# VectorE's SBUF passes ahead of its PSUM passes, GpSimd's pieces beside the latter, in a basic block's convolutions

## The chip, the core and the metric

The kernel runs on one core of a Trainium2 chip. The metric is the device time of one execution in microseconds. TensorE (PE) multiplies matrices into PSUM; PEld is its loading of weights. VectorE (DVE), ScalarE (ACT) and GpSimd (POOL) work element by element; SyncE (SP) issues most of the transfers. Each engine goes through its own list of instructions in order, and instructions on different engines wait for each other by semaphores.

## The reference

An input x of 2 images, 128 channels, 128 x 128 pixels, float32, goes through four layers: a 3x3 convolution followed by a small Mamba scan over channel groups, group norm and a residual (layer 0); a density gate (layer 1); layer 0's form again with other weights (layer 2); and a basic block with signs of weights (layer 3). Only the last is touched by the change:

```python
w1b = w1 + lax.stop_gradient(jnp.sign(w1) - w1)
w2b = w2 + lax.stop_gradient(jnp.sign(w2) - w2)
out = jax.nn.relu(_batchnorm(_conv3x3(x, w1b), gamma1, beta1))
out = _batchnorm(_conv3x3(out, w2b), gamma2, beta2)
out = out + x
return jax.nn.relu(out)
```

Batch norm takes mean and variance over both images and all pixels, so the second convolution can't begin before the first is complete.

## The kernel before, in words

Channels lie on the 128 partitions. The first 6900 us or so are layers 0 to 2. Then comes the basic block, the function `_basic_block`. It keeps the whole result of a convolution, Y, in SBUF (2 x 128 x 128 floats per partition), and runs over 32 bands of 8 rows (16 per image).

A band is convolved by Winograd's method along the rows: four output rows come from six input rows, so six transformed inputs, each convolved along the width with three taps, give four outputs. Four parts of the code do this for a band k:

- `edges(k)`: from the ten rows of the band (tile `band`, in one of three fixed buffers, `room`), VectorE makes four combinations (L889, each "-4 times one row set plus another", both inputs in SBUF) into slots 0, 3, 2 and 5 of a new tile `comb` (three buffers). GpSimd makes the differences: L890 into slots 1 and 4 out of the band, L891 into slots 0 and 5 out of the four combinations, L892 into slot 3.
- `rest_of(v)`: VectorE finishes `comb` in place with L897 (slot 4 from 1 and 4), L898 (slot 1, reading what L897 wrote) and L899 (slot 2, reading slot 3 of L892), all inputs in SBUF.
- `products(v)`: TensorE multiplies the six slots by the transformed weights u, 18 matmuls in the program (36 in the trace, L906), into a PSUM tile m of three banks (two buffers).
- `conv(m, ...)`: ScalarE copies a third of m to SBUF (c, L917). VectorE forms sums and differences of m and c (two L921, two L922, one pair into an SBUF tile and one pair into a PSUM tile, both named sd), and then the output rows in Y: L926 from m and the SBUF pair, and L927 to L930, each with the PSUM pair as one operand and an SBUF tile as the other. Two bn_stats passes over Y (L932) end it.

In L897 to L899 and L889 both inputs lie in SBUF; in L921 to L930 one lies in SBUF and the other in PSUM; L932 has a single input in SBUF.

`convolve(load, make, n)` runs this for one convolution, as a pipeline over steps k with the order of every engine written out by hand (a block of `tc.manual_schedule`). Step k holds, before the change: the rest of band k+1 (`rest_of`), the products of band k, the conv of band k-1, the load of band k+4, the making of band k+3, and the edges of band k+2 with their differences. The arguments load and make differ by convolution:

- In the first, `load` sets a border row to zero by a GpSimd memset where the image ends (L879, L881), and SyncE issues two transfers, the scan's output y into `band` (L974) and the layer's input into `xs` (L976, two buffers). `residual` makes the band: Silu with the group norm's scale and bias on ScalarE (L982), the residual's addition on GpSimd (L983, two SBUF inputs), and a transfer of the sum to `x3` in DRAM by SyncE (L984).
- In the second there is nothing to load. `normalised` sets the border, lets GpSimd copy two rows from the band before (L995), and ScalarE applies batch norm's scale and bias with a Relu to rows of Y (L997).

A third loop after both, the output pass, loads x3, adds the second convolution's result (L1010), applies Relu (L1011) and stores. It isn't touched.

Of the kernel before, what the change touches and what calls it, by code (L numbers as in the profile page):

```python
# [27 lines left out]
ALU = mybir.AluOpType  # L28
# [14 lines left out]
BAND = 8  # L43
# [776 lines left out]
def _basic_block(tc, src, y, norm, x3, scratch, w1, w2, bn, out, B, H):  # L820
# [7 lines left out]
    nc = tc.nc  # L828
    fours = BAND // 4
    with tc.tile_pool(name="bb", bufs=1) as cp, tc.tile_pool(name="bband", bufs=2) as bp, tc.tile_pool(  # L830
# [3 lines left out]
        def combined():  # L834
            return bp.tile([P, 6, fours, P + 2], F32, tag="comb", name="comb", bufs=3)
# [33 lines left out]
        bands = [(b, r0) for b in range(B) for r0 in range(0, H, BAND)]  # L869

        def span(k):

            r0 = bands[k][1]
            return room[k % 3], 1 if r0 == 0 else 0, BAND + 1 if r0 + BAND == H else BAND + 2
# [8 lines left out]
        def edges(k):  # L883

            xb = span(k)[0]
            v = combined()
            low, high = [xb[:, n : n + BAND, :].rearrange("p (i n) w -> p n i w", n=4) for n in (0, 2)]
            for n, at in enumerate((0, 3, 2, 5)):
                nc.vector.scalar_tensor_tensor(v[:, at], low[:, n], -4.0, high[:, n], ALU.mult, ALU.add)  # L889
            nc.gpsimd.tensor_tensor(v[:, 1:5:3], high[:, 1:3], low[:, 1:3], ALU.subtract)  # L890
            nc.gpsimd.tensor_tensor(v[:, 0:6:5], v[:, 2:6:3], v[:, 0:4:3], ALU.subtract)  # L891
            nc.gpsimd.tensor_tensor(v[:, 3], v[:, 2], v[:, 3], ALU.add)  # L892
            return v

        def rest_of(v):
            x = [v[:, n].rearrange("p i w -> p (i w)") for n in range(6)]
            nc.vector.scalar_tensor_tensor(x[4], x[1], -2.0, x[4], ALU.mult, ALU.add)  # L897
            nc.vector.scalar_tensor_tensor(x[1], x[1], 4.0, x[4], ALU.mult, ALU.add)  # L898
            nc.vector.scalar_tensor_tensor(x[2], x[2], 2.0, x[3], ALU.mult, ALU.subtract)  # L899

        def products(v):

            m = pp.tile([P, 3, 2, fours, P], F32, tag="m", name="m")
            for n, i in enumerate((2, 4, 3, 1, 0, 5)):
                for kw in range(3):
                    nc.tensor.matmul(  # L906
                        m[:, n // 2, n % 2],
                        lhsT=u[:, i, kw, :],
                        rhs=v[:, i, :, kw : kw + P],
                        start=(kw == 0),  # L910
                        stop=(kw == 2),
                    )
            return m

        def conv(m, b, r0, stats):
            c = bp.tile([P, 2, fours, P], F32, tag="c", name="c")
            nc.scalar.copy(c, m[:, 0])  # L917
            sd1 = bp.tile([P, 2, fours, P], F32, tag="sd", name="sd", bufs=1)
            sd2 = pp.tile([P, 2, fours, P], F32, tag="sd", name="sd")
            for n, sd in enumerate((sd1, sd2)):  # L920
                nc.vector.tensor_tensor(sd[:, 0], m[:, 1, n], c[:, n], ALU.add)  # L921
                nc.vector.tensor_tensor(sd[:, 1], m[:, 1, n], c[:, n], ALU.subtract)  # L922
            rows = Y[:, b, r0 : r0 + BAND, :]
            y = rows.rearrange("p (i n) w -> p n i w", n=4)
            (s1, d1), (s2, d2) = [(sd[:, 0], sd[:, 1]) for sd in (sd1, sd2)]
            nc.vector.tensor_tensor(y[:, 0:4:3], m[:, 2], sd1, ALU.add)  # L926
            nc.vector.scalar_tensor_tensor(y[:, 1], d2, 2.0, d1, ALU.mult, ALU.add)  # L927
            nc.vector.scalar_tensor_tensor(y[:, 2], s2, 4.0, s1, ALU.mult, ALU.add)
            nc.vector.tensor_tensor(y[:, 0], s2, y[:, 0], ALU.add)
            nc.vector.scalar_tensor_tensor(y[:, 3], d2, 8.0, y[:, 3], ALU.mult, ALU.add)  # L930
            for n in range(BAND // ROWS):
                nc.vector.bn_stats(  # L932
                    stats[:, (b * H + r0) // ROWS + n, :],
                    rows[:, n * ROWS : (n + 1) * ROWS, :].rearrange("p r w -> p (r w)"),
                )

        def affine(stats, n):
            mv = cp.tile([P, 2], F32, tag=f"mv{n}", name="mv")
            nc.vector.bn_aggr(mv, stats.rearrange("p a b -> p (a b)"))
            rstd = _rstd(nc, cp, mv[:, 1:2], BN_EPS, f"bn{n}")  # L940
            return _affine(nc, cp, mv[:, 0:1], rstd, bnc[:, 2 * n : 2 * n + 1], bnc[:, 2 * n + 1 : 2 * n + 2], f"bn{n}")
# [4 lines left out]
        def convolve(load, make, n):  # L946

            stats = cp.tile([P, B * H // ROWS, 6], F32, tag="st", name="st")
            v = {}
            E = mybir.EngineType  # L950
            with tc.manual_schedule(engines={E.PE, E.Activation, E.DVE, E.Pool, E.SP}):
                m = {}
                for k in range(-4, len(bands) + 1):
                    if 0 <= k + 1 < len(bands):
                        rest_of(v[k + 1])
                    if 0 <= k < len(bands):
                        m[k] = products(v.pop(k))
                    if k >= 1:
                        conv(m.pop(k - 1), *bands[k - 1], stats)
                    for ahead, f in ((4, load), (3, make)):  # L960
                        if 0 <= k + ahead < len(bands):
                            f(k + ahead)
                    if 0 <= k + 2 < len(bands):
                        v[k + 2] = edges(k + 2)
            return affine(stats, n)

        rests = {}
# [10 lines left out]
        def residual(k):  # L978
# [5 lines left out]
            nc.sync.dma_start(out=x3[b][:, r0 : r0 + BAND, :], in_=xb[:, 1 : BAND + 1, 1 : P + 1])  # L984

        s1, t1 = convolve(load, residual, 0)


# [11 lines left out]

        nc.sync.dma_start(out=u.rearrange("p a t c -> p (a t c)"), in_=later)
        s2, t2 = convolve(lambda k: None, normalised, 1)

        for k, (b, r0) in enumerate(bands):
# [90 lines left out]
```

## Time and profile before

The median of three runs is 7705.66 us (7701.60 to 7708.43). The profiled execution took 7677.97 us, and its span from the first to the last instruction is 7676.1 us, at a mean granted TensorE clock of 0.926.

| stretch of the span, us | what | PE busy | DVE busy | POOL busy | ACT busy | granted clock | GB/s |
|---|---|---|---|---|---|---|---|
| 0 to 7676.1 | all | 6354.0 | 7120.0 | 5563.7 | 4278.8 | 0.926 | 230 |
| 6900 to 7274 | first convolution | 278.5 | 343.9 | 201.5 | 65.9 | 0.90 | 165 |
| 7274 to 7575 | second convolution | 258.9 | 273.2 | 127.4 | 55.7 | 0.96 | 6 |
| 7575 to 7676 | output pass | 0 | 43.5 | 0 | 36.4 | 0.50 | 306 |

Some durations in the basic block, means from the groups by shape: L889 420 ns, L897 422, L921 413, L926 680, L932 685 on VectorE; L890 1451, L891 1406, L892 801, L983 2692 on GpSimd. The three L897 to L899 have the same shape as L889.

How to read it: busy time counts an instruction from its start to its end, also when it stands still in between, so the mean of a group against that of another of the same shape tells whether it does. In a group's row, after the shapes and the count, stand the busy time in us, the mean in ns, and after the second bar the idle time of the engine just before these instructions, with what ended it. In the timeline the columns are the start, the duration, engine, line, operation, and tiles; in brackets the engine's idle time before it and what it waited for.

### The profile page before, as it was taken

Reading aid. Unit: us, or ns where it says so; the run is one execution under the profiler, and the core shown is the slowest. Engines: PE = TensorE matmul, PEld = TensorE weight load, DVE = VectorE, ACT = ScalarE, POOL = GpSimd, SP = SyncE. Lnnn points to the kernel's source line nnn. Section 1 sums busy time; section 2 is a strip of 40 time slices with the busy share of each in tenths; the row PEclk is TensorE's granted clock in tenths of the full one; section 3 lists DMA queues with packets and bytes.
Section 4 is the critical chain, followed back from the end, with each engine's and each line's share of the span. In section 5 each row is a group of like instructions: output and inputs, shape, how many; then the busy total and the mean of one; then the engine's idle time right before and its main releaser. Section 6 shows DMA issues by size and latency. Waiting matters only on the chain.

```text
span 7676.1 us, 89472 instructions
## 1 busy us (share of the span) xinstructions
PE 6354.0 (83%) x30416; PEld 2345.8 (31%) x30416; DVE 7120.0 (93%) x7082; ACT 4278.8 (56%) x4877; POOL 5563.7 (72%) x1815
## 2 busy tenths in 40 slices
PE   7888888888888888867888888888888888877793
PEld 2222222222222222234222222222222222226673
DVE  6999999999999999966899999999999999999996
ACT  5666666666665666555566666666566666641112
POOL 5777877778777787743877777777777888765541
PEclk9999999999999999868999999999999999988897
DMA  7999999999999999944999999999999999975404
GB/s 207 252 248 249 254 251 255 245 249 250 253 247 248 252 252 254 246 180 150 245 258 246 246 251 248 254 249 248 246 252 249 248 256 255 251 201 181 129 1 170
DMA packets 573737, 1769.79 MB, mean 231 GB/s; under 512 B 85568, under 2 KB 239712, under 8 KB 458208
## 3 DMA queue, kind: packets, MB, share of 16 engines
q1 hardware_dynamic: 568672, 1747.28, 86.6%
q10 hardware_dynamic: 4608, 16.78, 0.6%
q8 instruction: 242, 3.96, 0.2%
q14 instruction: 215, 1.76, 0.1%
HBM read 1552.83 MB, written 210.89 MB: 230 GB/s over the span
## 4 chain that ended last, share of the span: by engine, by line
DVE 49%; DMA 22%; PE 12%; issue 7%; ACT 4%; POOL 4%; SPq 1%; POOLq 0%; DVEq 0%; ACTq 0%
DMA bcr<-sb 16%; DVE set L472 15%; DVE h L477 13%; DVE r L473 12%; DMA ur<-su 3%; PE set L454 2%; PE one L350 2%; POOL h L445 2%; ACT set L463 2%; PE one L400 2%; PE ys L492 1%; DVE v L505 1%; DVE comb L899 1%; PE ys L483 1%; POOL comb L891 1%
## 5 line engine op out<-in xcount | busy, mean ns | idle before, releaser
L445 POOL TENSOR_TENSOR h<-ur,bcr 128x2048 f32<-128x2048 f32 x896 | 4060.2, 4539 | 1141.8 <-DMA bcr<-sb 951.9
L472 DVE TENSOR_TENSOR set<-set,h 128x1024 f32<-128x1024 f32 x1792 | 2192.9, 1224 | 263.5 <-ACT set L463 161.8
L473 DVE TENSOR_TENSOR r<-set,bcr 128x1024 f32<-128x1024 f32 x1792 | 2194.1, 1224 | 61.4
L463 ACT ACTIVATE set<-set 128x1024 f32<-128x1024 f32 x1792 | 1746.3, 1006 | 887.1 <-PE set L454 876.1
L477 DVE TENSOR_TENSOR h<-set,h 128x1024 f32<-128x1024 f32 x1536 | 1864.0, 1214 | 24.0 <-POOL h L445 23.6
L454 PE MATMUL set<-dt,rep 32*128 32x512 f32 x7168 | 1405.3, 674 | 102.3 <-DVE h L477 96.1
L492 PE MATMUL ys<-r,ct 128*32 128x512 f32 x7168 | 1175.3, 635 | 35.6 <-DVE r L473 35.5
L323 PE MATMUL one<-band,conv 128*128 128x512 f32 x2304 | 1081.2, 605 | 22.0 <-DMA band<-in_x_dram 12.6
L454 PEld LDWEIGHTS set<-dt,rep 32*128 32x128 f32 x7168 | 404.3, 193 | 1002.7 <-issue 458.5
L400 PE MATMUL one<-xc,keep 128*64 128x512 f32 x1008 | 322.4, 723 | 457.6 <-ACT xc L357 355.8
L906 PE MATMUL m<-comb,u 128*128 128x256 f32 x2304 | 537.4, 394 | 137.3 <-DVE Y L926 90.8
L323 PEld LDWEIGHTS one<-band,conv 128*128 128x128 f32 x2304 | 406.5, 189 | 668.3 <-issue 596.7
L483 PE MATMUL ys<-t,ct 128*128 128x512 f32 x512 | 325.8, 722 | 251.9 <-DVE v L505 250.4
L906 PEld LDWEIGHTS m<-comb,u 128*128 128x128 f32 x2304 | 449.8, 197 | 224.6 <-issue 100.3
L492 PEld LDWEIGHTS ys<-r,ct 128*32 128x32 f32 x7168 | 181.7, 112 | 938.9 <-issue 767.5
L352 ACT ACTIVATE xc<-one,keep 128x512 f32<-128x512 f32 x252 | 173.4, 688 | 513.3 <-PE one L350 508.3
L374 POOL TENSOR_TENSOR u<-dt,xc 128x1024 f32<-128x1024 f32 x128 | 302.8, 2366 | 130.8 <-ACT dt L368 130.5
L420 PE MATMUL one<-prod,ct 128*128 128x512 f32 x504 | 278.1, 634 | 98.2 <-POOL prod L412 63.2
L350 PE MATMUL one<-y,w_in 128*128 128x512 f32 x504 | 343.1, 770 | 1.6 <-ACT xc L352 1.6
L463 ACT ACT_TABLE_LOAD x254 | 325.9, 1283 | 4.5
L917 ACT COPY c<-m 128x512 f32<-128x512 f32 x64 | 37.5, 586 | 517.9 <-PE m L906 292.2
L364 PE MATMUL one<-xc,w_dt 128*128 128x512 f32 x504 | 312.1, 704 | 2.7 <-ACT bc L407 2.7
(166 smaller groups left out, 6323.9 us busy)
## 6 DMA issues: line engine op xcount, KB each, us to landing
ur<-su SPq DMA_DIRECT2D x896, 896.0 KB, 11.4
bcr<-sb SPq DMA_DIRECT2D x896, 448.0 KB, 11.5
ur<-su SPq DMA_DIRECT2D x896, 128.0 KB, 11.0
su<-u SPq DMA_DIRECT2D x1024, 64.0 KB, 3.3
sb<-bc SPq DMA_DIRECT2D x256, 224.0 KB, 2.6
bcr<-sb SPq DMA_DIRECT2D x896, 64.0 KB, 10.7
y<-o SPq DMA_DIRECT2D x128, 256.0 KB, 9.1
band<-in_x_dram SPq DMA_DIRECT2D x28, 640.0 KB, 11.0
```

The source lines that it names most:

```text
L323: nc.tensor.matmul(py.rearrange("p (r w) -> p r w", r=ROWS), lhsT=w["conv"][:, tap, :], rhs=xb[:, r + kh : r + kh + ROWS, kw : kw + P], st ...
L350: nc.tensor.matmul(p, lhsT=w[("in", "z")[i]][:, g, :], rhs=s["y"], start=True, stop=True)
L400: nc.tensor.matmul(p[g * NQ * DS : (g + 1) * NQ * DS, :], lhsT=w[("xb", "xcm")[i]], rhs=s["xc"][:, g, :], start=True, stop=True,)
L445: nc.gpsimd.tensor_tensor(b, s["ur", t], s["bc", t][:, 0].unsqueeze(1).to_broadcast([P, NJ, NS]), ALU.mult)
L454: nc.tensor.matmul(a[j // 2][:, j % 2, :], lhsT=w["rep"][r, q, :], rhs=s["dt"][r, g, :], start=True, stop=True, tile_position=(r.start, 0),)
L463: nc.scalar.activation(x, x, AF.Exp)
L472: nc.vector.tensor_tensor(pt, pt, s["h", t - 1][:, js, :], ALU.mult)
L473: nc.vector.tensor_tensor(s["r", t][:, js, :], pt, s["bc", t - 1][:, 1].unsqueeze(1).to_broadcast([P, 2, NS]), ALU.mult)
L477: nc.vector.tensor_tensor(s["h", t][:, js, :], pt, s["h", t][:, js, :], ALU.add)
L483: nc.tensor.matmul(s["ys", g], lhsT=con["ident"], rhs=s["t1"][:, g, :], start=True, stop=False)
L492: nc.tensor.matmul(s["ys", g][a : a + NQ * DJ, :], lhsT=red[:, q, :], rhs=r[:, j, :], start=False, stop=(q == NQ - 1), tile_position=(0, a),)
L906: nc.tensor.matmul(m[:, n // 2, n % 2], lhsT=u[:, i, kw, :], rhs=v[:, i, :, kw : kw + P], start=(kw == 0), stop=(kw == 2),)
```

## The change

In `convolve`, the edges of band k+2 move from the end of a step to just behind the rest of band k+1, ahead of the products and the conv. GpSimd's three differences are taken out of `edges` into a function of their own, `differences`, which is called after the conv and ahead of the load and the making; inside it, the difference over the band alone (L890) comes last instead of first. So VectorE's order in a step becomes L897, L898, L899, four times L889, then L921 to L932; GpSimd's becomes L891, L892, L890, then border and L983 (or L995). Nothing is computed differently.

```diff
             for n, at in enumerate((0, 3, 2, 5)):
                 nc.vector.scalar_tensor_tensor(v[:, at], low[:, n], -4.0, high[:, n], ALU.mult, ALU.add)
-            nc.gpsimd.tensor_tensor(v[:, 1:5:3], high[:, 1:3], low[:, 1:3], ALU.subtract)
+            return v
+
+        def differences(k, v):
+            xb = span(k)[0]
+            low, high = [xb[:, n : n + BAND, :].rearrange("p (i n) w -> p n i w", n=4) for n in (0, 2)]
             nc.gpsimd.tensor_tensor(v[:, 0:6:5], v[:, 2:6:3], v[:, 0:4:3], ALU.subtract)
             nc.gpsimd.tensor_tensor(v[:, 3], v[:, 2], v[:, 3], ALU.add)
-            return v
+            nc.gpsimd.tensor_tensor(v[:, 1:5:3], high[:, 1:3], low[:, 1:3], ALU.subtract)
...
                     if 0 <= k + 1 < len(bands):
                         rest_of(v[k + 1])
+                    if 0 <= k + 2 < len(bands):
+                        v[k + 2] = edges(k + 2)
                     if 0 <= k < len(bands):
                         m[k] = products(v.pop(k))
                     if k >= 1:
                         conv(m.pop(k - 1), *bands[k - 1], stats)
+                    if 0 <= k + 2 < len(bands):
+                        differences(k + 2, v[k + 2])
                     for ahead, f in ((4, load), (3, make)):
                         if 0 <= k + ahead < len(bands):
                             f(k + ahead)
-                    if 0 <= k + 2 < len(bands):
-                        v[k + 2] = edges(k + 2)
```

## The prediction

> **What bounds the kernel now.** The page gives VectorE (DVE) 93% of the span busy, the most of all engines, and the changed functions run in its last five slices. So I cut it to these: the busy time of each engine over the first convolution, the second, and the output pass (columns: stretch, length, busy us of PE, PEld, DVE, ACT, POOL with instruction counts, granted clock, DMA share, GB/s).
>
> ```profile
> 6900.00:7274.00 374.00, 278.48 (x1152) 231.25 (x1152) 343.89 (x597) 65.89 (x67) 201.53 (x136) 0.90 0.52 165
> 7274.00:7575.00 301.00, 258.92 (x1152) 218.54 (x1152) 273.19 (x587) 55.66 (x65) 127.38 (x129) 0.96 0.02 6
> ```
>
> DVE is busy for 92% and 91% of the two convolutions. Whether it works or stands in a lock shows in the groups by shape, here from 6945 to 7255 us (count, busy us, mean ns):
>
> ```profile
> L899 DVE SCALAR_TENSOR_TENSOR comb<-comb 128x260 f32<-128x260 f32 x28 | 71.6, 2557 | 17.6 <-POOL comb L892 17.6
> L889 DVE SCALAR_TENSOR_TENSOR comb<-band 128x260 f32<-128x260 f32 x116 | 41.5, 420 | 0.0
> L898 DVE SCALAR_TENSOR_TENSOR comb<-comb 128x260 f32<-128x260 f32 x28 | 39.1, 1397 | 1.0
> L897 DVE SCALAR_TENSOR_TENSOR comb<-comb 128x260 f32<-128x260 f32 x28 | 11.8, 422 | 0.0
> ```
>
> One operation, one shape, and 420, 1397 or 2557 ns. The timeline of one step says why:
>
> ```profile
> 7026.42 1.40 POOL L891 TENSOR_TENSOR comb<-comb 128x520 f32<-128x520 f32 x1 [4.98 <-DVE comb L889]
> 7026.71 1.40 DVE L898 SCALAR_TENSOR_TENSOR comb<-comb 128x260 f32<-128x260 f32 x1
> ...
> 7027.90 0.80 POOL L892 TENSOR_TENSOR comb<-comb 128x260 f32<-128x260 f32 x1
> 7028.66 2.67 POOL L983 TENSOR_TENSOR band<-band,xs 128x1280 f32<-128x1280 f32 x1
> 7028.73 2.89 DVE L899 SCALAR_TENSOR_TENSOR comb<-comb 128x260 f32<-128x260 f32 x1 [0.63 <-POOL comb L892]
> ...
> 7031.30 1.47 POOL L890 TENSOR_TENSOR comb<-band 128x520 f32<-128x520 f32 x1
> ...
> 7031.55 0.41 DVE L921 TENSOR_TENSOR sd<-m,c 128x256 f32<-128x256 f32 x1
> ```
>
> L898 ends 0.29 us after POOL's L891, L899 0.29 us after POOL's L983: each stood still until GpSimd was done. L921, with one operand in PSUM, takes its usual 0.41 us beside L890. One step at the image border shows the other passes beside the long L983:
>
> ```profile
> 7051.49 2.90 POOL L983 TENSOR_TENSOR band<-band,xs 128x1280 f32<-128x1280 f32 x1
> ...
> 7053.22 0.68 DVE L926 TENSOR_TENSOR Y<-m,sd 128x512 f32<-128x512 f32 x1
> ```
>
> L926's mean is 680 ns, so nothing was lost; the next L890 ran over L929, L930 and L932, which took 0.41, 0.41 and 1.29 for the pair, as always. There L899 came 0.08 us ahead of L983, and that step took 8.88 us instead of 11.34. In the second convolution TensorE waits a little in each step:
>
> ```profile
> 7442.57 8.01 PE L906 MATMUL m<-comb,u 128*128 128x256 f32 x36 [1.04 <-DVE Y L926]
> 7451.61 8.01 PE L906 MATMUL m<-comb,u 128*128 128x256 f32 x36 [1.03 <-DVE Y L926]
> ```
>
> So a step is 11.34 us in the first convolution and 9.04 in the second, set by DVE with its stalls; TensorE needs 8.01.
>
> **What the Trainium skill says.** "SBUF — State Buffer", section "Who interferes with whom": a DVE instruction with two SBUF inputs contends with a GpSimd instruction that reads SBUF, and whichever issues second is blocked until the first ends; with at most one SBUF input (outside the two-port modes) it doesn't contend. The trace agrees: 2.89 us for L899 against L983's 2.67, and 0.41 for L921. "TensorE: Matmul & The Clock Gate", Part 1: idleness throttles the matrix clock. The trace agrees in kind: after idle gaps of about 3.3 us a step's 36 matmuls took up to 9.7 or 10.75 us, after gaps of 1.67 us or less always 8.01.
>
> **The change, part by part.** No instruction is added or removed; the order on DVE and POOL and the neighbours change. Start-to-start spacings on DVE, from the timeline: four L889 1.35 us, L897 to the L898 that reads it 0.46, L898 and L899 0.34 each uncontended, and a whole conv (L921 to the end of its place) 4.69. Sum 7.18. The rest of 11.34 is stall: L898 and the wait for L892 take 2.02 instead of 0.34, L899 2.82 instead of 0.34, together 4.16. In the second convolution L899 meets only the short L995, and the stalls are 1.86.
>
> *Edges ahead of conv, differences beside it.* Let E be the end of the four L889. POOL then starts L891 0.08 later (as now), L892 1.49 after that, L890 0.76 later, and after 1.45 the add L983 (2.67): it ends at E+6.45. DVE meanwhile runs conv from E-0.08 to E+4.62, all passes with at most one SBUF input, so nothing is lost by the overlap. The former stalls of L898 and the 0.63 wait for L892 are gone.
>
> *What is late next, first convolution.* The add L983 now lies behind all three differences, and DVE reaches L897 at E+4.62, while L983 holds the read port until E+6.45. So 1.83 us of stall remain. L897 ends 0.30 after L983 (as L899 does now), then 0.04, 0.34, 0.34 and 1.43 to the new E: 6.45+0.30+2.15 = 8.90 us a step. Edges must also wait for this L983 now (before, its band was finished 16 us earlier): it is the same instant, no further cost. The loop is DVE edges, POOL differences and add, DVE rest and edges.
>
> *TensorE in it.* L926 ends at E+2.06 and frees PSUM for products at E+2.2; 8.01 fits in 8.90 with 0.9 idle, short of what cools the clock. There is one new wait: edges comes ahead in the step, so its buffer (one of three) is the one that products(k-1) has yet to give back. Queued behind edges on DVE is conv, which TensorE needs two products later. In the first convolution those matmuls end some 6 us before edges; costs nothing.
>
> *The queues.* On POOL the border memsets and the add go behind the differences; three memsets of 0.20 enter the chain, and three shorter adds give 0.7 back. On SP nothing is reordered, but the store of x3 and the next two loads now go out together at L983's end: store 3.2, y 4.3 and xs 5.5 us to landing now, 1.79 MB per step, 201 GB/s at 8.90 against 165 now and up to 255 elsewhere on the page. They are needed two steps later at E+3.8, some 15 us after issue, Silu's 1.46 included for y; even the slowest seen there (8.64) fits.
>
> *First convolution, sum.* Edges(0) ends about 6916 (a weight pass, L853, no longer stands behind the second add); three rounds of 8.90 bring E of band 3 to 6942.7 (now 6947.0), 28 more bring band 31 to 7191.9 (now 7255.2). The tail is longer, since edges leads by more: products(30) runs E+2.2 to 10.2, products(31) to 18.2, then copy 0.6 and conv 4.79: 23.7 us against 18.5. The statistics end at 7215.6 instead of 7273.7: 58.1 us saved.
>
> *Second convolution.* POOL needs 0.08+1.49+0.76+1.45+0.4, DVE 7.18, TensorE 8.01: TensorE becomes the bound. With T the end of products(k-1), edges runs T+0.1 to 1.5, conv's L926 ends at T+3.6, far ahead of T+8, and rest ends at T+7.3; the new buffer wait costs DVE 0.7 us of idleness a step and TensorE nothing. Now 284.3 us pass from the first matmul (7284.91) to the last (7569.21). After: first products 10.43 (cold, as now) plus 31 x 8.01 = 258.7, so 25.6 less; the first products start 0.9 later, because all three differences stand ahead of the first rest. Saved: 24.7.
>
> The output pass and all before 6900 us stay. Sum 82.8: span 7676.1 becomes 7593.3. The profiled execution took 7678.0, the median of the runs shown is 7705.7; I take the difference off the median: **7623 us**, 1.07% faster.
>
> What the trace doesn't show is a long stretch of matmuls with no gap. Its bounds: 8.01 x 31, or a clock a little lower, as the first 10.43 over 8.01 shows it can be; 8.4 a step would cost 12 us. I take 8.01, since from 7300 to 7320 TensorE is busy all 20 us at clock 1.00.
>
> **Rivals.**
> 1. *The first convolution keeps a longer loop* (landings late through SP, or matmuls that cool down): some 9.7 to 10.5 us a step, each added 1.0 taking back 29 us. Saved 37 to 60: 7645 to 7669. For it speaks that store and loads now share the DMA queues; against it the 5 us of slack.
> 2. *The add doesn't stall DVE* as reckoned, and TensorE's 8.01 binds both: 28 x 0.89 more, 107 saved, about 7598. Against it: L899 behind L983 in nearly every step now.
> 3. *Slower: conv's passes are held while GpSimd reads*. Then POOL's 6.45 and DVE's 4.69 and 2.49 come one after another: 13.6 a step, and 4.2+4.69+2.49 = 11.4 in the second; +64 and +69, about 7839. It decides once conv is held over 2.4 us a step in the first. L921, L926, L929, L930 and L932 beside POOL at their usual times speak against it; a wait written for a whole tile, which would do the same, can't be excluded.
> 4. *The change only moves the stall*: DVE loses behind L983 what it gains on L891. This would need 4 us of stall behind L983; it has only 2.67.
>
> **How the numbers follow.** My forecast 0.70 (own range 7608 to 7640: 0.3 us a step and startup each way), rival 1 0.14, rival 2 0.07, rival 3 0.06, rival 4 0.03 (no change). Within 0.2%, about 15 us, a measurement can't tell this kernel from no change. Faster 0.91, same 0.03, slower 0.06. The range takes in the forecast and most of rivals 1 and 2: 7598 to 7654.
>
> **What would show it.** L898 and L899 at 0.42 us; L897 at up to 2.2 us in the first convolution, ending 0.3 after L983; L889 starting every 8.9 us, then every 8.0; L921 to L932 unchanged; matmuls of the second convolution without gaps, clock 1.00. I am wrong if conv's passes lengthen beside POOL, if ACT's Silu waits for landings, or if L889 waits for L906 for over a microsecond in the first convolution.

## The result, and the profile after

The changed kernel took 7594.4 us (median of four runs, 7579.2 to 7596.2), the kernel before 7707.1 in the same comparison; the ratio is 0.9849, 95% interval 0.9832 to 0.9866. Repeated on one chip (first experiment below) it was 0.9882, 0.9867 to 0.9898: 97 us. The profiled execution took 7595.0 us, with a span of 7593.2.

The lines of `after` are shifted against before: L897 to L899 (rest) are now L901 to L903; the differences L891, L892, L890 are L895, L896, L897, in that order; conv's L921, L926 and L932 are L925, L930 and L936; the matmuls L906 are L910; the addition L983 is L989.

Stretches of the changed kernel, with the columns used before (length, busy us of PE, PEld, DVE, ACT, POOL, granted clock, DMA share, GB/s): first convolution, second convolution.

```profile
6900.00:7215.00 315.00, 265.44 (x1176) 221.53 (x1173) 293.03 (x620) 70.09 (x70) 189.84 (x136) 0.93 0.64 197
7215.00:7492.00 277.00, 253.69 (x1162) 221.34 (x1160) 239.08 (x598) 57.49 (x67) 115.34 (x129) 0.96 0.03 11
```

The groups by shape in the first convolution (6950 to 7190 us): count, busy us, mean ns, idle time ahead.

```profile
L989 POOL TENSOR_TENSOR band<-band,xs 128x1280 f32<-128x1280 f32 x26 | 69.8, 2684 | 0.0
L901 DVE SCALAR_TENSOR_TENSOR comb<-comb 128x260 f32<-128x260 f32 x28 | 51.5, 1840 | 3.5 <-POOL comb L897 3.5
L889 DVE SCALAR_TENSOR_TENSOR comb<-band 128x260 f32<-128x260 f32 x112 | 40.4, 423 | 0.0
...
L897 POOL TENSOR_TENSOR comb<-band 128x520 f32<-128x520 f32 x28 | 36.3, 1296 | 0.0
L895 POOL TENSOR_TENSOR comb<-comb 128x520 f32<-128x520 f32 x28 | 36.1, 1288 | 72.5 <-DVE comb L889 72.5
...
L902 DVE SCALAR_TENSOR_TENSOR comb<-comb 128x260 f32<-128x260 f32 x28 | 12.0, 429 | 1.0
L903 DVE SCALAR_TENSOR_TENSOR comb<-comb 128x260 f32<-128x260 f32 x28 | 11.8, 422 | 0.0
...
L933 DVE TENSOR_TENSOR Y<-sd,Y 128x256 f32<-128x256 f32 x27 | 11.2, 413 | 0.0
```

Where before two passes of the rest stood still (1397 and 2557 ns), now one does, the first, at 1840; the other two take 0.42 us. GpSimd's pieces became shorter too: L895 1288 ns against 1406, L897 1296 against 1451. One step in the timeline:

```profile
7082.32 2.68 POOL L989 TENSOR_TENSOR band<-band,xs 128x1280 f32<-128x1280 f32 x1
...
7083.48 1.81 DVE L901 SCALAR_TENSOR_TENSOR comb<-comb 128x260 f32<-128x260 f32 x1
...
7086.01 1.44 DVE L889 SCALAR_TENSOR_TENSOR comb<-band 128x260 f32<-128x260 f32 x4
...
7087.60 1.29 POOL L895 TENSOR_TENSOR comb<-comb 128x520 f32<-128x520 f32 x1 [2.59 <-DVE comb L889]
...
7088.97 0.73 POOL L896 TENSOR_TENSOR comb<-comb 128x260 f32<-128x260 f32 x1
...
7089.66 1.30 POOL L897 TENSOR_TENSOR comb<-band 128x520 f32<-128x520 f32 x1
...
7090.91 2.69 POOL L989 TENSOR_TENSOR band<-band,xs 128x1280 f32<-128x1280 f32 x1
...
7092.08 1.81 DVE L901 SCALAR_TENSOR_TENSOR comb<-comb 128x260 f32<-128x260 f32 x1
```

L901 starts 1.16 us after the addition starts and ends 0.29 us after it has ended: 7083.48+1.81 against 7082.32+2.68. From one L989 to the next pass 8.59 us. Conv's passes lie beside GpSimd's pieces and keep their times (L933 413 ns; the same pass, L929, had 412 before). In the second convolution TensorE has no gaps left; the timeline of PE shows all 32 products as one row:

```profile
7234.31 251.67 PE L910 MATMUL m<-comb,u 128*128 128x256 f32 x1152 [17.30 <-DVE comb L903]
```

I split the span at the last group norm's aggregation (L604) and at the two batch norms' aggregations. The part from L604 to the end, "the block", holds all that the change touches.

| us | ahead of the block | first convolution | second | output pass | block |
|---|---|---|---|---|---|
| before | 6891.6 | 382.2 | 300.9 | 101.4 | 784.5 |
| changed | 6909.9 | 312.6 | 269.0 | 101.7 | 683.3 |

The block is 101.2 us shorter. The part ahead, where both kernels do the same, is 18.3 us longer in this profile: so the spans differ by just 82.9 us, which is by chance the sum that the prediction had.

### The profile page after: what moved, and what is told of

It is laid out like the page before. It is cut to its first block, busy times and chain, and to the rows that moved or that the text cites. A ratio compares the mean times of both kernels' runs of the same rounds, so it can differ in the third digit from the quotient of the medians.

```text
span 7593.2 us, 89536 instructions
## 1 busy us (share of the span) xinstructions
PE 6291.6 (83%) x30416; PEld 2339.8 (31%) x30416; DVE 7026.3 (93%) x7082; ACT 4279.0 (56%) x4877; POOL 5538.6 (73%) x1815
## 4 chain that ended last, share of the span: by engine, by line
DVE 39%; DMA 30%; PE 14%; issue 6%; POOL 5%; ACT 4%; SPq 2%; POOLq 0%; DVEq 0%; ACTq 0%
DMA bcr<-sb 23%; DVE set L472 12%; DVE h L477 10%; DVE r L473 10%; DMA ur<-su 4%; PE m L910 4%; POOL h L445 3%; PE set L454 2%; PE one L350 2%; ACT set L463 2%; PE ys L492 1%; PE ys L483 1%; DVE v L505 1%; PE one L400 1%; DVE comb L901 1%
## 5 line engine op out<-in xcount | busy, mean ns | idle before, releaser
L454 PE MATMUL set<-dt,rep 32*128 32x512 f32 x7168 | 1385.9, 676 | 97.8 <-DVE h L477 93.5
L492 PE MATMUL ys<-r,ct 128*32 128x512 f32 x7168 | 1160.1, 634 | 33.0 <-DVE r L473 32.6
L910 PE MATMUL m<-comb,u 128*128 128x256 f32 x2304 | 510.2, 382 | 63.0 <-DVE comb L903 45.3
L910 PEld LDWEIGHTS m<-comb,u 128*128 128x128 f32 x2304 | 437.5, 191 | 135.4 <-issue 72.0
L421 ACT COPY t<-one 128x512 f32<-128x512 f32 x252 | 147.7, 586 | 326.9 <-PE one L420 326.9
L427 POOL TENSOR_TENSOR t<-t,xc 128x1024 f32<-128x1024 f32 x128 | 302.1, 2360 | 10.0
```

Source lines behind the costliest of these rows:

```text
L454: nc.tensor.matmul(a[j // 2][:, j % 2, :], lhsT=w["rep"][r, q, :], rhs=s["dt"][r, g, :], start=True, stop=True, tile_position=(r.start, 0),)
L492: nc.tensor.matmul(s["ys", g][a : a + NQ * DJ, :], lhsT=red[:, q, :], rhs=r[:, j, :], start=False, stop=(q == NQ - 1), tile_position=(0, a),)
L910: nc.tensor.matmul(m[:, n // 2, n % 2], lhsT=u[:, i, kw, :], rhs=v[:, i, :, kw : kw + P], start=(kw == 0), stop=(kw == 2),)
```

## The experiments

My theory: VectorE's passes with two SBUF inputs stand behind a GpSimd instruction that reads SBUF (they are recorded as busy but make no progress until it ends), those with one operand in PSUM don't, so that the change takes away most of the standing. One rival: it is a wait on semaphores, or the order alone. Another, since spans and medians differ by different amounts: the change reaches the layers ahead of the block too.

**Both kernels again, on one chip.** Neither is edited.

> The kernel before once more, beside itself. Theory A (the layers ahead of the basic block differ from one execution to the next and from chip to chip, whatever the kernel): ratio to the kernel before 1.000 within its interval, while the stretch ahead of the block (until the last group norm's aggregation, L604 at 6891.6 us in the first profile) lies anywhere from 6880 to 6925. Theory B (the first profile of before was ordinary, and the timed runs of before are slow for a reason in that kernel): the stretch is again 6890 within 5 us, in this profile too. The basic block itself, from there to the end, 784 us in both.

> The changed kernel once more, on the same chip as the repeated kernel before. Theory A: the basic block is 683 us again, 101 less than before (about 99 by its own chain), and the layers ahead of it are the same as those of before within run variation, so the gain is about 99 us, ratio 0.987. Theory B (the change also reaches layers 0 to 2, by placement or the like): the gain is again about 113, ratio 0.9853, and the stretch ahead of the block is about 14 us shorter than that of the repeated kernel before.

The kernel before against itself: 7685.9 us (14 runs, 7668.8 to 7702.5) and 7687.2 (19 runs, 7665.2 to 7701.6), ratio 0.9999, 0.9989 to 1.0010. The changed kernel: 7589.8 us, ratio 0.9882, 97 us. The profiles:

| us | ahead of the block | first convolution | second | output pass | block |
|---|---|---|---|---|---|
| before again | 6904.1 | 382.1 | 301.1 | 102.3 | 785.5 |
| changed again | 6925.0 | 312.4 | 269.2 | 101.5 | 683.1 |

The block repeats to 1 us, the part ahead doesn't: 6891.6 and 6904.1 for the one kernel, 6909.9 and 6925.0 for the other, and in the profiles below, which do the same there, from 6874.7 to 6939.9. Theory A holds: the gain is that of the block, 101 us, and 97 and 113 are two measurements of it through a spread of some 36 us in the executions of one kernel (101 of 7707 us is a ratio of 0.9869, inside the second interval and just beyond the end of the first). Theory B wanted 113 us again and a part ahead that is 14 us shorter; it was 97, and the part ahead was 21 us longer. Four profiles can't exclude a few us there.

**GpSimd writes and doesn't read, in the order of before.**

```diff
-            nc.gpsimd.tensor_tensor(v[:, 0:6:5], v[:, 2:6:3], v[:, 0:4:3], ALU.subtract)
+            for _ in range(2):
+                nc.gpsimd.memset(v[:, 0:6:5], 0.0)
...
-            nc.gpsimd.tensor_tensor(x, x, rests.pop(k), ALU.add)
+            nc.gpsimd.memset(x, 0.0)
+            nc.gpsimd.memset(x[:, :7], 0.0)
```

The other two differences are replaced in the same way.

> The order of the kernel before, but GpSimd's three differences and the residual's addition are replaced by memsets of about the same duration on the same slots, so that GpSimd waits and signals as before and writes SBUF but reads nothing (the differences and the residual are left out of the result). Theory (VectorE stands behind GpSimd's reading): L898 and L899 take 0.42 us, the 0.63 wait for L892's place stays or shrinks, a step falls from 11.34 and 9.04 to about 7.8 to 8.0 in both, where TensorE takes over. Rival (VectorE waits on semaphores or on any GpSimd access to SBUF): L899 still ends after the memsets that stand for the addition, and a step stays near 11.3 and 9.0.

The block took 683.0 us against 784.5, in the old order (297.7 and 282.0 in the convolutions). A step in the timeline (here L901 is the second pass of the rest, L902 the third, L986 a memset in place of the addition):

```profile
7046.35 1.12 POOL L893 MEMSET comb<- 128x520 f32 x2 [3.50 <-DVE comb L889]
7046.67 0.43 DVE L901 SCALAR_TENSOR_TENSOR comb<-comb 128x260 f32<-128x260 f32 x1
...
7048.04 1.17 POOL L986 MEMSET band<- 128x1280 f32 x1
7048.13 0.43 DVE L902 SCALAR_TENSOR_TENSOR comb<-comb 128x260 f32<-128x260 f32 x1 [1.04 <-POOL comb L895]
```

Both passes take 0.43 us beside GpSimd at work in the same tile and in the band. So it is GpSimd's reading that holds them, and neither a wait nor its writing: the theory holds, the rival falls. My size was off: the second pass now ends 1 us earlier, while slot 3 is ready only half a us earlier, so the wait for it grew from 0.63 to 1.04 us, and a step was 8.32 us, not 7.8 to 8.0. In the second convolution the third pass still took 0.59, behind the copy (L995 before, L999 here), which I had left reading, and a step was 8.48.

**The second pair in SBUF.** The same arithmetic, but conv's last four passes then have two SBUF inputs.

```diff
-            sd2 = pp.tile([P, 2, fours, P], F32, tag="sd", name="sd")
+            sd2 = bp.tile([P, 2, fours, P], F32, tag="sd2", name="sd2")
```

> The changed kernel with the second pair of sums and differences in SBUF instead of PSUM, so that conv's last four passes have two SBUF inputs each; the arithmetic is the same. Theory (a pass with one operand in PSUM escapes GpSimd's reading, one with two in SBUF stands behind it): these four (1.33 us a step uncontended) join the sum of those that hold the port, 8.59 becomes about 9.6 to 10 in the first convolution, and in the second VectorE's 7.2 plus one to 1.3 of standing passes TensorE's 7.8: 8.2 to 8.6. The block is 40 to 65 us longer than 683. Rival (where the operands lie doesn't matter, only which engine waits for which): no change.

The block took 772.4 us (379.0 and 289.9), 89 longer than the changed kernel's, where I expected 40 to 65: nearly the whole gain is gone. The timeline of a step in the first convolution:

```profile
7045.22 0.68 DVE L931 SCALAR_TENSOR_TENSOR Y<-sd,sd 128x256 f32<-128x256 f32 x1
...
7045.57 1.48 POOL L897 TENSOR_TENSOR comb<-band 128x520 f32<-128x520 f32 x1
...
7045.82 1.51 DVE L932 SCALAR_TENSOR_TENSOR Y<-sd,sd 128x256 f32<-128x256 f32 x1
7047.01 2.84 POOL L989 TENSOR_TENSOR band<-band,xs 128x1280 f32<-128x1280 f32 x1
7047.26 2.89 DVE L933 TENSOR_TENSOR Y<-sd,Y 128x256 f32<-128x256 f32 x1
```

Passes of 0.41 us became 0.68, 1.51 and 2.89, each behind one GpSimd piece, and each piece in turn behind a pass. That the operand lies in PSUM is what carries the change. A step was 10.9 us, beyond my 9.6 to 10: I had added only the passes themselves, but while L933 stands behind the addition, the statistics behind it, which have a single SBUF input, are held off too and find no GpSimd work left to run beside (GpSimd is idle for 4.58 us from the addition's end on). The second convolution's 8.65 a step (8.2 to 8.6 expected) shows the same.

**The other half alone.** The order of before, with only the band difference moved to the end of GpSimd's three.

> The other part alone: the order of the kernel before with the edges at the end of a step, and GpSimd's difference over the band last among the three. The rest, which follows the edges at once on VectorE, needs all three. Theory: GpSimd ends them 3.5 us behind the edges, takes the port for the addition at once (2.69), and VectorE ends its first rest pass 0.3 later; with 0.35, 0.34, conv's 4.69 and the edges' 1.36 that is some 13.2 us a step in the first convolution and 10.9 in the second, against 11.34 and 9.04: the block is 890 to 900 us against 785. Rival (the order of the differences is what brings the gain): the block is shorter than 785.

The block took 906.7 us, 122 longer than before (446.2 and 357.7). Its timeline, where L892 is the band difference and L897 the first pass of the rest:

```profile
7042.13 1.29 POOL L892 TENSOR_TENSOR comb<-band 128x520 f32<-128x520 f32 x1
7043.38 2.67 POOL L983 TENSOR_TENSOR band<-band,xs 128x1280 f32<-128x1280 f32 x1
...
7043.45 2.89 DVE L897 SCALAR_TENSOR_TENSOR comb<-comb 128x260 f32<-128x260 f32 x1 [3.53 <-POOL comb L892]
```

The step of 13.3 us came out as reckoned (13.2); the block is somewhat beyond the 890 to 900. In the old order this part of the change costs 122 us, because VectorE waits for the last difference (3.53 us) and then stands behind the addition. What it does in the new order, the next experiment shows.

**The band difference first, in the new order.** The edges stay ahead; L890's line goes back to the head of the three. So this is the change without its second part.

> The changed kernel with GpSimd's difference over the band alone (slots 1 and 4) first among the three, as it was before; the edges stay ahead of conv. It can then start as soon as the addition ends, where VectorE's rest and edges stand. Theory (those that hold the read port add up): in the first convolution the sum stays the same, 8.5 to 8.8 a step against 8.59; in the second, VectorE's 7.2 plus up to 1.3 of standing behind it pass TensorE's 7.8, so 8.2 to 8.5 a step, and the block (from the last group norm's aggregation to the end, 683 us in the changed kernel) is 12 to 25 us longer. Rival (only the place of the edges counts): the block stays at 683.

> The changed kernel with the difference over the band first, which one profile gave a block of 672.6 us against 683.2. Theory (that profile is right, and GpSimd's start-up is hidden behind VectorE's first rest pass): block 672 to 673 again, and timed beside the kernel before a ratio 0.9855 (111 us), within 0.0015. Rival (a single profile misled): the block is 683, ratio 0.987 as the changed kernel.

In the first of the two runs both my theory and its rival missed: the block got shorter, 672.6 us. In the second profile it was 671.2 (302.3 and 267.0), so the first was no stray. Timed, the ratio to before is 0.9832, 0.9817 to 0.9847, a larger gain than the 0.9855 that I expected. So the move of the edges alone takes 112 us off the block of before, and the other part of the change, the band difference last, gives 11 of them back: it is a loss in the new order as in the old. The timeline (L895 is now the band difference, the addition L989 lies ahead of it):

```profile
7044.95 2.69 POOL L989 TENSOR_TENSOR band<-band,xs 128x1280 f32<-128x1280 f32 x1
...
7047.44 0.48 DVE L901 SCALAR_TENSOR_TENSOR comb<-comb 128x260 f32<-128x260 f32 x1
...
7047.71 1.36 POOL L895 TENSOR_TENSOR comb<-band 128x520 f32<-128x520 f32 x1
7047.95 1.40 DVE L902 SCALAR_TENSOR_TENSOR comb<-comb 128x260 f32<-128x260 f32 x1
```

With one piece fewer ahead of it, the addition ends just as conv does, so the first pass hardly stands (0.48). The second stands behind the band difference, 0.97 us, where L901 stood 1.39 behind the addition; the step here is 8.23 instead of 8.59 (the median is 8.25). I had put the whole of a piece on VectorE's path. But the band difference began while L901 still ran (to 7047.92), so of its 1.36 us only 0.97 were added. In the second convolution the first pass stood 0.56 us (0.98 instead of 0.42) and not the 1.3 I expected; that used up the edges' wait for TensorE (0.48 in the changed kernel), and the step stayed 7.77.

**One difference more on VectorE, and both moves.** In the first convolution VectorE does the difference of slots 0 and 5 itself, behind the edges.

```diff
+            if n_conv == 0:
+                nc.vector.tensor_tensor(v[:, 0:6:5], v[:, 2:6:3], v[:, 0:4:3], ALU.subtract)
...
-            nc.gpsimd.tensor_tensor(v[:, 0:6:5], v[:, 2:6:3], v[:, 0:4:3], ALU.subtract)
+            if n_conv != 0:
+                nc.gpsimd.tensor_tensor(v[:, 0:6:5], v[:, 2:6:3], v[:, 0:4:3], ALU.subtract)
```

> The changed kernel, and in the first convolution VectorE does the difference of slots 0 and 5 as well, right behind the four edges (0.6 us there, 1.37 us taken off GpSimd). Theory (in the first convolution a step is the sum of those that hold the read port, GpSimd's 6.1 and VectorE's 2.5, with conv hidden): GpSimd then holds it for 4.8 behind the edges, hardly longer than conv's 4.7, and a step is 7.9 to 8.1 instead of 8.59; 28 steps save 14 to 19 us against the changed kernel. Rival (VectorE's own work sets the step): 0.6 more per step, 17 us slower than the changed kernel.

The block took 666.2 us (294.4 and 267.7), 17 less; timed 7572.4 us, ratio 0.9854 (0.9839 to 0.9869), beside the changed kernel's 0.9882 on the same chip. In the timeline the pass costs VectorE 0.70 us, and the first rest pass (L904) no longer stands:

```profile
7032.04 2.68 POOL L992 TENSOR_TENSOR band<-band,xs 128x1280 f32<-128x1280 f32 x1
...
7034.57 0.44 DVE L904 SCALAR_TENSOR_TENSOR comb<-comb 128x260 f32<-128x260 f32 x1
...
7037.20 0.70 DVE L891 TENSOR_TENSOR comb<-comb 128x520 f32<-128x520 f32 x1
```

More work on the busiest engine, and a shorter step (7.96 us): the theory's 14 to 19 us hold. With the band difference first as well:

> The changed kernel with GpSimd's difference over the band first among its pieces, and with the difference of slots 0 and 5 on VectorE in the first convolution. Each alone shortened the block of 683 us: to 672.6 and to 666.2. Theory (TensorE's 7.8 a step is close by then): the two don't add up; the first convolution, 312.5 us in the changed kernel and 302.5 and 294.4 in the two, comes to 285 to 293, the second stays at 267, and the block is 655 to 664; the kernel is 20 to 28 us faster than the changed one. Rival (VectorE is the bound by then, and standing behind the band difference adds to its 7.8): 8.3 us a step, first convolution 300 to 305, block 670 to 676.

The block took 664.9 us (295.5 and 266.8), ratio 0.9829 (0.9815 to 0.9843). The moves don't add up; the first convolution is no shorter than with the one, 8.0 us a step, between my two figures. The timeline shows what sets it: VectorE hardly idles, 0.14 us a step. From one first rest pass to the next (7058.40 to 7066.40) its spacings are 1.20 for the rest, 1.48 for the edges, 0.62 for the moved piece and 4.70 for conv, 8.00 in all. So VectorE is the bound there, as the rival had it, but with almost no standing (L904 takes 0.48 us, L905 0.43). This version has the lowest median, 7562.3 us, beside 7567.2 for the band difference first alone on that chip; their intervals don't tell them apart.

**The addition only writes.** In the changed kernel two memsets stand for the residual's addition, as above.

> The changed kernel with the residual's addition in the first convolution replaced by two memsets of the same band (1.17 and 0.85 us in an earlier run), which write and don't read; the residual is left out. Theory (in the first convolution VectorE stands behind the addition's reading): the first rest pass takes 0.42 us instead of 1.80, and a step falls from 8.59 to TensorE's 7.8; 28 steps save about 22 us, and the block is 660 to 663. Rival (VectorE waits for the addition because the edges need its band): the edges wait instead, and a step is only as much shorter as the memsets are than the addition, 0.65 us, 7.95, with the rest pass at 0.42 and a wait ahead of the edges.

The block took 657.2 us, the first convolution 285.0 against 312.6. Two rows of the timeline:

```profile
7040.98 0.41 DVE L901 SCALAR_TENSOR_TENSOR comb<-comb 128x260 f32<-128x260 f32 x1
...
7042.67 1.45 DVE L889 SCALAR_TENSOR_TENSOR comb<-band 128x260 f32<-128x260 f32 x4 [0.48 <-PE m L910]
```

The first pass takes 0.41, and the edges wait for TensorE: a step is 7.77 us. They don't wait for the band: the second memset ended in the median step 0.80 us before the edges began, which is more than the 0.67 us by which the memsets (1.17 and 0.85) are shorter than the addition (2.69). The stall left in the changed kernel was the addition's reading, as the theory had it.

## Why the prediction was right or wrong

The direction, the mechanism and its places were right; the time was wrong. I forecast 7623 us with a range from 7598; it was 7594.4. The step that failed is the pricing: GpSimd's three differences and TensorE's product were put too long, and with them the step of both convolutions. Against the prediction's own terms:

- **Conv hidden beside GpSimd: right.** L925 to L936 kept their times (L925 421 ns against 413, L930 680, L936 685), and the second pair in SBUF shows on what that rests.
- **The stall moves to the first rest pass, behind the addition: right in place, too large in size.** From VectorE's arrival at L901 to the addition's end I had 1.83 us; it was 1.52 (7092.08 to 7090.91+2.69). The 0.31 between them is the next point's.
- **A step of 8.90 in the first convolution: 8.59 (8.58 in the mean).** The sum's terms were 0.08, 1.49, 0.76, 1.45, 2.67, 0.30, 2.15; measured 0.15, 1.37, 0.69, 1.25, 2.69, 0.29, 2.15. The three differences were mis-sized. I had taken their spacings from steps in which they themselves stood behind VectorE: a mean of 1451 ns for L890, though rows of the trace before had it at 1.29 where nothing was in its way. Over 28 steps 9.0 us. What the order of the three differences costs, the prediction never weighed: with the band difference first, a step is 8.25.
- **Start and tail.** E, the end of the edges, of band 3 came 48.9 us after the aggregation instead of 51.1; the tail was 23.5 against 23.7. With the steps, 312.6 instead of 324.0.
- **The second convolution, TensorE bound: right, at 7.78 a product and not 8.01.** 8.01 is a burst from its first start to its last end, and holds the end of the last matmul, which the next product overlaps. All 32 took 251.7 us, not 258.7: 7.0 us. The prediction said that the trace of before shows no long stretch of matmuls without a gap; it does, the first six products of the second convolution:

```profile
7284.91 49.26 PE L906 MATMUL m<-comb,u 128*128 128x256 f32 x216 [16.67 <-DVE comb L899]
```

Less the cold first product's 10.43 that is 38.83 us for five, 7.77 each, so the right price lay there. The other effect that was forecast, edges waiting for TensorE, was there, 0.48 us a time, and cost TensorE nothing (us in all, times, longest):

```profile
DVE comb L889 <- PE m L910: 12.1, 25, 0.8
```

- **The clock: right.** It is 1.00 from 6950 to 7190 and from 7250 to 7470, where it was 0.90 to 0.97 in the first convolution before.
- **Landings: harmless, as reckoned.** y and xs landed in 5.8 and 6.8 us (medians, 4.3 and 5.5 before). Silu waited for y, 43 us in all over 25 steps, which the prediction had named as a sign of being wrong; but the addition behind it never waited, so the sign was badly chosen. (The page of before has slices of up to 258 GB/s, not 255.)

Together the block is 18.4 us shorter than reckoned: 83 forecast, 101 measured. With 101.2 in place of its 82.8 it would have said 7604.5. The rest of the 28.6 us that 7594.4 lies below 7623 is the level of the runs: 113 was measured at first, 97 on one chip, around the block's 101. The prediction took three runs within 7 us of each other for the spread of this kernel, though its own profiled execution lay 28 us off their median; nineteen runs of before cover 36 us. So beside the pricing of GpSimd's and TensorE's pieces, the range failed too, since it left out the spread of layers that the change doesn't touch. None of the rivals occurred. The time lies near rival 2's 7598, but that is chance: the addition does stall VectorE, and where it doesn't (the run in which it only writes), the block is 657 us. The 0.2% that I took for the bound of no change is about the half-width of the intervals here (0.0015), so it was fair.

## What to carry to other kernels

When the same pass shows several durations in a profile, look for the GpSimd instruction that it ends just behind; then put VectorE's passes with two SBUF inputs together, and lay GpSimd's reading pieces beside those with an operand in PSUM. Measure the parts of a change apart: here one part brought 112 us and the other took 11 back. Take prices for the sum from rows in which nothing stands in the way, and price a burst of matmuls by the spacing of bursts that touch. A busy engine can gain from taking work over, if that frees what it stands behind.

## What was not expected of the hardware

- Standing behind the other engine works both ways and in turns: with the second pair in SBUF, GpSimd's L897 took 1.48 us instead of 1.30, and VectorE's passes 0.68, 1.51 and 2.89.
- A pass that stood behind a GpSimd piece ended 0.28 to 0.30 us after it, whether it had stood for 1 us (L898 before) or for 2.5 (L899).
- In one kernel, executions spread over 36 us. In the profiles the part ahead of the block, the same in all kernels, went from 6874.7 to 6939.9 us, while a block that was profiled twice repeated within 1.4 us. What causes it stays open; no run here was made for it.
